# Broadcasting a softmax maximum: a transfer to all partitions and a ScalarE copy to PSUM instead of a VectorE shuffle

## The chip, the cores and the metric

The kernel runs on one core of one Trainium2 chip, all of it in 32-bit floats. The metric is the device time of one execution in microseconds (us). A core has several engines that work beside each other, each on its own list of instructions in a fixed order: TensorE (PE; its weight loads are shown apart as PEld) for matmuls and transposes, VectorE (DVE), ScalarE (ACT) and GpSimd (POOL) for elementwise work, and SyncE (SP), which here issues the transfers (DMAs). An engine waits where the next instruction in its list needs something that another engine or a transfer has not finished. SBUF is the memory with 128 partitions that all of them read and write. PSUM is the smaller memory into which TensorE writes; VectorE and ScalarE read and write it too.

## What is computed

The reference is a network of two layers over 16 batches of 64 latent vectors of 128 numbers. Each layer adds three things to the latents `x`:

```python
x = x + L0_xattn(ctx_1024, layernorm(x), ...)   # cross-attention: 16 heads of 64, 1601 context rows a batch
x = x + L0_attn(layernorm(x), ...)              # a selective scan over the 64 latents, state 16
x = x + L0_ffn(layernorm(x), ...)               # small attention over heads, then 8 experts, 2 taken, and a shared one
x = x + L1_xattn(ctx_1024, layernorm(x), mask, ...)   # the same attention with a mask over the context
x = x + L1_attn(layernorm(x), ...)              # convolution and a scan with a state of 64
x = x + L1_ffn(layernorm(x), ...)               # a gated feed-forward with both operands rounded to 4-bit blocks
```

The cross-attention, where most of the time goes, is

```python
q  = ln_latents @ Wq
kv = concat([ln_context, ln_latents]) @ Wkv     # 1601 + 64 keys
w  = softmax(q k^T * scale (+ mask))            # per head, over 1665 keys
x += (w @ v) @ Wo
```

A softmax over 1665 keys needs, for each query, the largest score before the exponentials are taken: `exp(s - max)`.

## The kernel before

**Groups and steps.** The projections of keys and values are folded into the queries and the output, so that the keys are the normalised context itself. The attention is cut into 64 groups, one for each layer, batch and half of the heads; a group has 8 heads of 64 queries, that is 512 columns (`NQ`). The 1600 first context rows and the 64 latents make 13 key tiles (`NT`) of up to 128 rows; context row 1601 is handled apart. A step is one key tile of one group, and the steps of all groups follow each other without a break: 64 x 13 of them, about 29.8 us for the 13 of one group.

In each step `scores` issues one matmul of 128 keys by 512 queries into one of three PSUM buffers `s` (L726). VectorE folds it into a running maximum `R` (128x512) with L734 (masked, layer 1) or L736 (layer 0). ScalarE copies it to an SBUF buffer `st` (L739 or L741). These buffers hold two tiles each, and there are 13 pairs of them (`PAIRS`). The exponentials come later, once the group's maximum is known: `weigh` subtracts the maximum `mb` from one pair on VectorE (L834) and takes the exponential on ScalarE (L835). `LAG` = 23 steps after a score step, `average` multiplies its weights with the values (`av`, L847, 128 queries by 129 columns, the last column being the sum of the weights). The second pair of query blocks runs one step after the first.

**From `R` to `mb`.** `R` holds, for each of 128 rows of a key tile, the maximum per query; what is left is the maximum over the 128 partitions, the same number wanted on every partition. The tuple `plan` says at which step after a group's last score (its offset) each part of that is issued:

- offset 0, `partial`: VectorE reduces `R` with a transpose in blocks of 32 into 128x16 (`part`). A second instruction (L772) joins it with the score of the apart row (`sx`) into `four`, four copies side by side, 128x64.
- offset 2, `joint`: TensorE transposes `four`, VectorE reduces it to `top`, 64x32: the 512 maxima, four times.
- offset 3, `handed`: two transfers on SyncE, `top` into every 32nd partition of `R`, and a quarter of `top` into DRAM (`mdram`).
- offset 5, `everywhere`: VectorE's stream_shuffle (L793) spreads partition 0 of each 32 over its block, from `R` into PSUM (`mb`).
- offset 7, `own_max`: a transfer reads `mdram` back as one number for each query on the partition of that query, `m4`.
- offset 11, `apart_weight`: VectorE takes `df` = score of the apart row minus `m4` (L807), ScalarE its exponential `ee`.
- offset 12, `apart_part`: GpSimd multiplies the apart row's values (`xeb`) by `ee` into `aq`, to which `gather` later adds the averages.

`weigh` begins at offset `WAIT` = 6 and takes one of the seven pairs every second step. The scores of the apart row are made for two batches at a time by `apart_scores`: VectorE copies them to `se`, adds the mask in layer 1, and spreads them into the four-fold `sx` (L477). The last group of all has another path (`maximum`, `spread_max`), and ends in `finish`.

**The other work.** It is cut into generators that hand back control after a few instructions, by `yield` with a number (a cost, charged against a budget per step) or with `HOP1`, `HOP`, `HOP3`, `HOP5` (wait 1, 2, 3 or 5 steps). A list `prep` holds what must be ready at a step: folding of weights (`fold_qk`, `fold_vo`), normalised latents, queries, and `context`, which loads and normalises a batch's context. `context` also makes its transposed form in layer 0: ScalarE writes a scaled copy into a staging tile `kts` (one buffer), and a transfer takes it to DRAM (`xhT`). `blocks` stages a group's transposed result in another tile of the same size, `tq`. A list `between` holds the scan and feed-forward of each layer (`scan0`, `moe`, then `scan1`, `ffn`), run one at a time; the first may begin `LAG` + 11 steps after the score steps that it depends on began. `scan1` and `ffn` of layer 1 run over chunks of 128 latents (two batches): chunks 0-1, 2-3, 4-5, 6 and 7. In `scan1`, for each of the chunks, four products of `bT` and `cT` go to PSUM (`gr`, L1405), from which VectorE makes `gm` (L1408).

**What sets the order.** `scores` records its own instructions on each engine (`place`). Work issued under `behind()` is ordered after the newest of these on its engine, or the one before it. A scheduler then settles the final order on each engine from the dependences, these additional ones, and its own model; every engine executes that order as it stands. SyncE issues all transfers in its order, and a transfer whose data is not ready holds those behind it. After the last group, `upto_sums` takes what is first in `between` (the last chunk but one) to the sum at the end of its `ffn`; `finish` closes the last group; and the remaining generators run alternately (`tails`). The last chunk's attention output is summed at L930, its scan's projection at L1051, its feed-forward at L1560. `fill` adds matmuls without use to keep TensorE busy there.

## Time and profile before

| what | us |
|---|---|
| median of three runs | 1907.09 |
| the three runs | 1906.38, 1907.09, 1911.22 |
| the profiled execution's own time | 1906.72 |
| its span on the engines | 1905.0 |
| TensorE (PE) busy | 1856.2 (97%) |
| VectorE (DVE) busy | 1654.1 (87%) |
| ScalarE (ACT) busy | 1325.3 (70%) |
| GpSimd (POOL) busy | 582.0 (31%) |
| granted TensorE clock, mean | 0.997 |
| bytes by DMA | 145.16 MB |

The profile is one execution, recorded by the hardware. The span runs from the first to the last instruction, and the execution's own time has 1.7 us around it. "Busy" is the sum of the time in which an engine executes; weight loads overlap matmuls. In lines on single instructions, L736 is a line of the kernel's code, the names are output and inputs, "128x512 f32" is partitions by elements. In square brackets or after `<-` stands how long the engine was idle just before, and which engine's instruction ended that wait. The granted clock says at which share of its full speed TensorE was allowed to run. The page's costliest groups are these (busy time and mean ns of one, then idle time before, and what ended it):

```profile
L847 PE MATMUL av<-kv,st 128*128 128x129 f32 x6656 | 886.4, 276 | 4.0 <-DVE aq L853 1.9
L726 PE MATMUL s<-qT,kvT 128*128 128x512 f32 x1664 | 863.0, 601 | 19.9 <-ACT st L741 9.6
L835 ACT ACTIVATE st<-st 128x1024 f32<-128x1024 f32 (+1 forms) x448 | 444.3, 995 | 123.8 <-DVE st L834 120.9
L834 DVE TENSOR_TENSOR st<-st,mb 128x1024 f32<-128x1024 f32 (+1 forms) x448 | 503.5, 1130 | 1.8 <-PE mb L821 1.1
L739 ACT ACTIVATE st<-s,mcol 128x512 f32<-128x512 f32 x416 | 283.0, 683 | 229.6 <-DVE R L734 213.6
L741 ACT COPY st<-s 128x512 f32<-128x512 f32 x416 | 238.9, 580 | 93.2 <-DVE R L736 87.7
```

The two attention matmuls take 1749 of TensorE's 1856 us. VectorE's subtraction of `mb` (L834) is its largest item with 503.5 us.

### The profile page before, as it was taken

Reading aid. Unit: us, or ns where it says so; the run is one execution under the profiler, and the core shown is the slowest. Engines: PE = TensorE matmul, PEld = TensorE weight load, DVE = VectorE, ACT = ScalarE, POOL = GpSimd, SP = SyncE. Lnnn points to the kernel's source line nnn. Section 1 sums busy time; section 2 is a strip of 40 time slices with the busy share of each in tenths; the row PEclk is TensorE's granted clock in tenths of the full one; section 3 lists DMA queues with packets and bytes.
Section 4 is the critical chain, followed back from the end, with each engine's and each line's share of the span. In section 5 each row is a group of like instructions: output and inputs, shape, how many; then the busy total and the mean of one; then the engine's idle time right before and its main releaser. Section 6 shows DMA issues by size and latency. Waiting matters only on the chain.

```text
span 1905.0 us, 32600 instructions
## 1 busy us (share of the span) xinstructions
PE 1856.2 (97%) x11494; PEld 1398.6 (73%) x11494; DVE 1654.1 (87%) x3124; ACT 1325.3 (70%) x2575; POOL 582.0 (31%) x657
## 2 busy tenths in 40 slices
PE   9999999999999999999998999999999999999997
PEld 5677777677777767777676777767777777787786
DVE  6998787998888998986999988999888987988974
ACT  5789888897878888765665756767655665665651
POOL 5222223653214553221453311455210222202110
PEclk9999999999999999999999999999999999999999
DMA  6132333442235442242433322333332132212100
GB/s 195 43 82 72 78 78 98 109 94 68 57 96 115 98 90 70 77 131 64 94 89 73 78 61 52 102 86 71 78 81 64 34 77 54 55 41 61 39 18 23
DMA packets 395886, 145.16 MB, mean 76 GB/s; under 512 B 251455, under 2 KB 386379, under 8 KB 395723
## 3 DMA queue, kind: packets, MB, share of 16 engines
q1 hardware_dynamic: 395178, 142.82, 31.4%
q8 instruction: 91, 1.49, 0.3%
q14 instruction: 73, 0.59, 0.1%
q10 hardware_dynamic: 544, 0.26, 0.0%
HBM read 97.66 MB, written 43.79 MB: 74 GB/s over the span
## 4 chain that ended last, share of the span: by engine, by line
PE 56%; DVE 9%; issue 4%; DMA 3%; ACT 1%; POOL 1%; SPq 0%; DVEq 0%; POOLq 0%; ACTq 0%
PE av L847 22%; PE s L726 21%; DVE R L734 2%; PE o L926 2%; DVE st L834 2%; PE q L518 2%; DVE h L1027 1%; PE gu L1175 1%; PE me L1160 1%; PE gu L1174 1%; DVE R L736 1%; DMA kv<-xh 1%; PE sb L1361 1%; DMA xhT<-kts 1%; DMA bb<-bcd 1%
## 5 line engine op out<-in xcount | busy, mean ns | idle before, releaser
L847 PEld LDWEIGHTS av<-kv,st 128*128 128x128 f32 x6656 | 870.3, 192 | 364.5 <-issue 343.8
L847 PE MATMUL av<-kv,st 128*128 128x129 f32 x6656 | 886.4, 276 | 4.0 <-DVE aq L853 1.9
L726 PE MATMUL s<-qT,kvT 128*128 128x512 f32 x1664 | 863.0, 601 | 19.9 <-ACT st L741 9.6
L835 ACT ACTIVATE st<-st 128x1024 f32<-128x1024 f32 (+1 forms) x448 | 444.3, 995 | 123.8 <-DVE st L834 120.9
L834 DVE TENSOR_TENSOR st<-st,mb 128x1024 f32<-128x1024 f32 (+1 forms) x448 | 503.5, 1130 | 1.8 <-PE mb L821 1.1
L739 ACT ACTIVATE st<-s,mcol 128x512 f32<-128x512 f32 x416 | 283.0, 683 | 229.6 <-DVE R L734 213.6
L741 ACT COPY st<-s 128x512 f32<-128x512 f32 x416 | 238.9, 580 | 93.2 <-DVE R L736 87.7
L734 DVE SCALAR_TENSOR_TENSOR R<-s,mcol,R 128x512 f32<-128x512 f32 x352 | 260.6, 740 | 46.4 <-PE s L726 45.3
L736 DVE TENSOR_TENSOR R<-s,R 128x512 f32<-128x512 f32 x352 | 239.8, 681 | 64.7 <-PE s L726 63.0
L726 PEld LDWEIGHTS s<-qT,kvT 128*128 128x128 f32 x1664 | 254.4, 191 | 41.5 <-ACT st L741 18.3
L644 POOL TENSOR_TENSOR kv<-kv,vec 128x384 f32<-128x384 f32 (+1 forms) x128 | 133.5, 1059 | 200.6 <-PE kt L705 85.1
L892 POOL TENSOR_TENSOR aq<-aq,rd 128x512 f32<-128x512 f32 x63 | 71.7, 1138 | 191.0 <-DVE rd L891 122.5
L1033 POOL TENSOR_TENSOR sc_y<-sc_y,h 128x512 f32<-128x512 f32 x60 | 79.4, 1323 | 127.5 <-DVE h L1032 110.5
L1016 POOL TENSOR_TENSOR db<-sc_u,bb 128x512 f32<-128x512 f32 x64 | 83.5, 1307 | 80.9 <-DVE h L1027 74.1
L1027 DVE TENSOR_TENSOR_SCAN h<-da,db 128x512 f32<-128x512 f32 x64 | 91.8, 1434 | 2.3 <-POOL db L1016 2.3
L695 ACT ACTIVATE kv<-kv,coff,crstd 128x128 f32<-128x128 f32 x182 | 78.7, 492 | 1.5 <-POOL coff L692 1.3
L815 POOL TENSOR_TENSOR aq<-xeb,ee 128x516 f32<-128x516 f32 x63 | 66.8, 1060 | 32.9 <-ACT ee L808 32.8
L686 ACT ACTIVATE scr<-kv,cmean 128x128 f32<-128x128 f32 x182 | 72.6, 399 | 3.9 <-DVE cmean L682 2.1
L641 POOL MEMSET kv<- 128x13 f32 x30 | 3.7, 125 | 218.9 <-PE av L847 218.1
L518 PE MATMUL q<-xnT,wqk 128*128 128x128 f32 x512 | 67.9, 276 | 1.0 <-ACT qT L527 0.7
L518 PEld LDWEIGHTS q<-xnT,wqk 128*128 128x128 f32 x512 | 62.6, 192 | 3.8 <-issue 1.4
L139 POOL TENSOR_TENSOR crstd<-cvar,neghalf 128x13 f32<-128x13 f32 x14 | 34.2, 2440 | 101.3 <-DVE cvar L690 101.1
(433 smaller groups left out, 1877.5 us busy)
## 6 DMA issues: line engine op xcount, KB each, us to landing
bb<-bcd SPq DMA_DIRECT2D x64, 256.0 KB
aTd<-tq SPq DMA_DIRECT2D x248, 64.0 KB
aT<-aTd SPq DMA_DIRECT2D x62, 256.0 KB
xh<-kv SPq DMA_DIRECT2D x16, 832.0 KB
kv<-xh SPq DMA_DIRECT2D x16, 832.0 KB
kvT<-xhT SPq DMA_DIRECT2D x16, 800.0 KB
kv<-in_ctx_dram SPq DMA_DIRECT2D x15, 768.0 KB
xhT<-kts SPq DMA_DIRECT2D x45, 256.0 KB
```

Source lines behind the costliest of these rows:

```text
L518: nc.tensor.matmul(t[:, k * P:(k + 1) * P], self.wqk[:, g * 4 + k, :], xnT, start=True, stop=True)
L644: nc.gpsimd.tensor_tensor(kv[:, lo:hi, :D], kv[:, lo:hi, :D], self.row(self.vec[:, w1, :], [P, hi - lo, D]), ALU.mult)
L726: mm = nc.tensor.matmul(s, self.kv_of[lay, b][1][:, i * P:(i + 1) * P], q, start=True, stop=True)
L734: mx = nc.vector.scalar_tensor_tensor(R, s, mc, last, ALU.add, ALU.max)
L736: mx = nc.vector.tensor_tensor(R, s, last, ALU.max)
L739: ev = nc.scalar.activation(st, s, AF.Identity, bias=mc)
L741: ev = nc.scalar.copy(st, s)
L834: nc.vector.tensor_tensor(st, st, self.row(mb, [P, n, NQ]), ALU.subtract)
L835: nc.scalar.activation(st, st, AF.Exp)
L847: nc.tensor.matmul(grp["av", j][:, k, :], st, self.kv_of[lay, b][0][:, i, :], start=(i == 0 and k == 0), stop=(i == NT - 1 and k == 1))
L1016: nc.gpsimd.tensor_tensor(db, u, self.row(bb[:, 0], both), ALU.mult)
L1027: nc.vector.tensor_tensor_scan(flat(h), flat(da), flat(db), 0.0, ALU.mult, ALU.add)
```

## The change

- `four` becomes `joined`, 128x16 instead of 128x64, and `top` has 16 rows instead of 64 (two buffers).
- `handed` moves from offset 3 to 2 and only writes `top` to `mdram`. The transfer into `R` is gone, and `R` has one buffer instead of two.
- `everywhere` moves from offset 5 to 2. It is now a transfer that reads the 512 numbers of `mdram` into all 128 partitions of a new SBUF tile `wide` (256 KB, one buffer).
- a new part, `settle`, at offset 6: ScalarE copies `wide` to the PSUM tile `mb`. The stream_shuffle is gone.
- `own_max` moves from offset 7 to 4. `df` becomes a part of its own, `apart_below`, at offset 9 and on GpSimd; `apart_weight` at 11 is only the exponential.
- `sx`, and in layer 1 the mask's addition to `se`, move from VectorE to GpSimd.
- `weigh` begins one step later (`WAIT` 7), `average` too (`LAG` 24), and with `LAG` the start of the work in `between`.
- `fold_vo`'s sum over the heads (L366) is made in four pieces, one step apart.
- `kts` and `tq` share one tag with two buffers.
- `scan1` hands back for two more steps (`HOP`) after the `gr` products of each chunk, except in the last scan.

```diff
--- before.py
+++ after.py
@@ -52,8 +52,8 @@
 NEG = -1.0e30
 NT = G + 1
 NQ = 512
-LAG = 23
-WAIT = 6
+LAG = 24
+WAIT = 7
 PAIRS = 13
 BLK = 32
 LOWEST = -3.0e38
@@ -363,7 +363,9 @@
         raw = lambda name: self.at.tile([P, D], F32, tag="raw", name=f"{name}{lay}", bufs=3)
         ws, b = raw("ws"), raw("b1r")
         nc.gpsimd.tensor_copy(b, self.vcol[:, b1:b1 + 1].to_broadcast([P, D]))
-        nc.vector.tensor_reduce(ws, self.wvo.rearrange("p h d -> p d h"), AX.X, ALU.add)
+        for lo in range(0, D, 32):
+            nc.vector.tensor_reduce(ws[:, lo:lo + 32], self.wvo[:, :, lo:lo + 32].rearrange("p h d -> p d h"), AX.X, ALU.add)
+            yield HOP1
         yield HOP
         t = self.tp(f"cb{lay}")
         nc.tensor.matmul(t[:, :D], b, ws, start=True, stop=True)
@@ -471,10 +473,10 @@
             for i in range(2):
                 nc.vector.tensor_copy(se[i * L:(i + 1) * L, :], mine[:, i])
             if lay:
-                nc.vector.tensor_scalar(se, se, self.mex[:, 2 * c + j:2 * c + j + 1], None, ALU.add)
+                nc.gpsimd.tensor_scalar(se, se, self.mex[:, 2 * c + j:2 * c + j + 1], None, ALU.add)
             sx = self.sm([P, H // 2, 4], "sx")
             shape = [P, H // 2, 4]
-            nc.vector.tensor_tensor(sx, self.bc(se, shape), self.row(self.own, shape), ALU.add)
+            nc.gpsimd.tensor_tensor(sx, self.bc(se, shape), self.row(self.own, shape), ALU.add)
             self.se_of[lay, 2 * c + j] = se, sx
         yield 0.6
@@ -703,7 +705,7 @@
                 t = self.tp(f"kt{b}_{g}")
                 for k in range(4 * g, min(4 * g + 4, n)):
                     nc.tensor.transpose(t[:, (k - 4 * g) * P:(k - 4 * g + 1) * P], kv[:, k, :D], self.ident)
-                raw = self.at.tile([P, 512], F32, tag="kts", name=f"kts{b}_{g}", bufs=1)
+                raw = self.at.tile([P, 512], F32, tag="kts", name=f"kts{b}_{g}", bufs=2)
                 for to, by in ((kvT[:, g * 512:g * 512 + w], w1), (raw[:, :w], YG1)):
                     nc.scalar.activation(to, t[:, :w], AF.Copy, scale=self.vcol[:, by:by + 1])
                 nc.sync.dma_start(out=self.xhT[b][:, g * 512:g * 512 + w], in_=raw[:, :w])
@@ -716,7 +718,7 @@
         lay, b, half = grp["key"]
         if i == 0:
             grp["st"] = []
-            grp["R"] = self.at.tile([P, NQ], F32, tag="R", name=f"R{g}", bufs=2)
+            grp["R"] = self.at.tile([P, NQ], F32, tag="R", name=f"R{g}", bufs=1)
         if i % 2 == 0:
             n = min(2, NT - i)
             grp["st"].append(self.at.tile([P, n, NQ], F32, tag=f"st{n}", name=f"st{g}_{i // 2}", bufs=PAIRS if n == 2 else 2))
@@ -767,30 +769,34 @@
         lay, b, half = grp["key"]
         sx = self.se_of[lay, b][1][:, half * 4:half * 4 + 4, :].rearrange("p k f -> p (k f)")
         t = grp["turn"] = self.tp(f"tm{g}")
-        part, four = t[:, P:P + 16], self.sm([P, 4, 16], "four", bufs=2)
+        part, joined = t[:, P:P + 16], self.sm([P, 16], "joined")
         nc.vector.tensor_reduce(part, grp["R"].rearrange("p (c j) -> p c j", j=BLK), AX.X, ALU.max, apply_transpose=True)
-        nc.vector.tensor_tensor(four, self.row(part, [P, 4, 16]), self.row(sx, [P, 4, 16]), ALU.max)
-        grp["four"] = four.rearrange("p r c -> p (r c)")
+        nc.vector.tensor_tensor(joined, part, sx, ALU.max)
+        grp["joined"] = joined
     def joint(self, g):
         nc, grp = self.nc, self.groups[g]
         t = grp.pop("turn")
-        nc.tensor.transpose(t[:64, :P], grp["four"], self.ident)
-        top = grp["top"] = self.sm([64, BLK], "top")
-        nc.vector.tensor_reduce(top, t[:64, :P].rearrange("c (a j) -> c j a", j=BLK), AX.X, ALU.max)
+        nc.tensor.transpose(t[:16, :P], grp["joined"], self.ident)
+        top = grp["top"] = self.sm([16, BLK], "top", bufs=2)
+        nc.vector.tensor_reduce(top, t[:16, :P].rearrange("c (a j) -> c j a", j=BLK), AX.X, ALU.max)
     def handed(self, g):
-        nc, grp = self.nc, self.groups[g]
-        nc.sync.dma_start(out=grp["R"][0:P:BLK, :], in_=grp["top"])
-        nc.sync.dma_start(out=self.mdram[g], in_=grp["top"][:16])
+        grp = self.groups[g]
+        self.nc.sync.dma_start(out=self.mdram[g], in_=grp["top"])
     def everywhere(self, g):
+
+        wide = self.groups[g]["wide"] = self.at.tile([P, NQ], F32, tag="wide", name=f"wide{g}", bufs=1)
+        self.nc.sync.dma_start(out=wide, in_=self.mdram[g].rearrange("c j -> (c j)").partition_broadcast(P))
+
+    def settle(self, g):
         grp = self.groups[g]
         grp["mb"] = self.tp(f"mb{g}")
-        self.nc.vector.stream_shuffle(grp["mb"], grp["R"], [0] * BLK)
+        self.nc.scalar.copy(grp["mb"], grp.pop("wide"))
     def own_max(self, g):
@@ -799,14 +805,18 @@
         with nc.allow_non_contiguous_dma(reason="one number for each query"):
             nc.sync.dma_start(out=m4, in_=self.mdram[g].rearrange("(k f) j -> (f j) k", k=4))
+    def apart_below(self, g):
+
+        grp = self.groups[g]
+        lay, b, half = grp["key"]
+        df = grp["df"] = self.sm([P, 4], "df")
+        self.nc.gpsimd.tensor_tensor(df, self.se_of[lay, b][0][:, half * 4:half * 4 + 4], grp["m4"], ALU.subtract)
+
     def apart_weight(self, g):
-        nc, grp = self.nc, self.groups[g]
-        lay, b, half = grp["key"]
-        df, ee = self.sm([P, 4], "df"), self.sm([P, 4], "ee")
-        nc.vector.tensor_tensor(df, self.se_of[lay, b][0][:, half * 4:half * 4 + 4], grp["m4"], ALU.subtract)
-        nc.scalar.activation(ee, df, AF.Exp)
-        grp["ee"] = ee
+        grp = self.groups[g]
+        ee = grp["ee"] = self.sm([P, 4], "ee")
+        self.nc.scalar.activation(ee, grp.pop("df"), AF.Exp)
     def apart_part(self, g):
@@ -894,7 +904,7 @@
     def blocks(self, g):
         nc, aq = self.nc, self.groups[g]["aq"]
-        t = self.at.tile([P, NQ], F32, tag="tq", name=f"tq{g}", bufs=1)
+        t = self.at.tile([P, NQ], F32, tag="kts", name=f"tq{g}", bufs=2)
         nc.vector.transpose(t.rearrange("p (k d) -> p k d", k=4), aq[:, :, :D])
         for i in range(P // BLK):
             to = self.aTd[g].rearrange("(j r) (k i c) -> i r k j c", r=BLK, i=P // BLK, c=BLK)[i]
@@ -1407,6 +1417,8 @@
                     gi = gm[c].rearrange("p (k i) t -> p i k t", i=2)[:, i]
                     nc.vector.tensor_tensor(gi, gs[i][:, :2 * L].rearrange("p (k t) -> p k t", k=2), self.row(self.upto, [P, 2, L]), ALU.mult)
                 yield 0.6
+                if not last:
+                    yield HOP
             for c in range(CG):
                 sg = self.tp(f"seg{c}")
                 for h in range(NH):
@@ -1570,7 +1582,7 @@
         self.groups = [{"key": (lay, b, half)} for lay in range(2) for b in range(NB) for half in range(2)]
         ng = len(self.groups)
         self.plan = (
-            ((0, self.partial), (2, self.joint), (3, self.handed), (5, self.everywhere), (7, self.own_max), (11, self.apart_weight), (12, self.apart_part)),
+            ((0, self.partial), (2, self.joint), (2, self.handed), (2, self.everywhere), (4, self.own_max), (6, self.settle), (9, self.apart_below), (11, self.apart_weight), (12, self.apart_part)),
             ((1, self.maximum), (3, self.spread_max)),
         )
         per_layer = NB * 2 * NT
```

## The prediction

> **What bounds the kernel now.** I read the page's busy times first, then stretches of the span, then the waits, then the two ends of the chain of waits.
>
> ```profile
> PE 1856.2 (97%) x11494; PEld 1398.6 (73%) x11494; DVE 1654.1 (87%) x3124; ACT 1325.3 (70%) x2575; POOL 582.0 (31%) x657
> ```
>
> TensorE is the bound almost throughout: 1856.2 of 1905.0 us. A change that leaves the matmuls alone (this one does: 5996 issued before and after) can win only from the other 49 us and from matmuls run slowly. Where is that time? The next fence is the table of stretches (us; then busy us of PE, its weight load, DVE, ACT, POOL; granted clock; DMA).
>
> ```profile
> 340.00:450.00 110.00, 106.14 (x630) 78.97 (x628) 107.25 (x170) 95.88 (x223) 61.60 (x55) 1.00 0.42 92
> 600.00:720.00 120.00, 113.41 (x666) 83.89 (x665) 114.01 (x173) 103.21 (x232) 64.36 (x59) 1.00 0.46 104
> 910.00:1050.00 140.00, 128.98 (x731) 92.30 (x730) 131.17 (x189) 86.55 (x142) 63.55 (x56) 0.99 0.35 77
> 1250.00:1320.00 70.00, 65.85 (x369) 46.88 (x368) 69.91 (x109) 48.22 (x77) 43.80 (x38) 1.00 0.44 93
> 1830.00:1905.00 75.00, 64.43 (x499) 55.48 (x498) 42.56 (x122) 19.97 (x42) 8.07 (x14) 1.00 0.09 22
> 1604.20:1607.60 3.40, 3.40 (x16) 1.86 (x14) 2.03 (x4) 2.23 (x4) 0.00 (x0) 0.50 0.27 43
> ```
>
> The first four are the stretches with `scan0` beside the attention: VectorE is 94 to 100% busy and TensorE idles 3.9+6.6+11.0+4.1 = 25.6 us. The fifth is the end, 10.6 us idle. The sixth is a stretch at half clock; the waits before it, and the waits that tie TensorE to VectorE:
>
> ```profile
> ACT st L739 <- DVE R L734: 213.6, 203, 3.5
> ACT st L741 <- DVE R L736: 87.7, 98, 3.2
> PE s L726 <- ACT st L741: 9.6, 17, 1.1
> 1602.76 0.31 PEld L1405 LDWEIGHTS gr<-sd_cT,sd_bT 64*64 64x64 f32 x8 [2.04 <-DVE gm L1408]
> 1721.90 0.51 PEld L1405 LDWEIGHTS gr<-sd_cT,sd_bT 64*64 64x64 f32 x16 [2.86 <-DVE gm L1408]
> ```
>
> A score matmul needs one of three PSUM buffers; ScalarE's eviction frees it and waits for VectorE's running maximum. So VectorE's backlog reaches TensorE through ScalarE. The two `gr` lines are `scan1`, second pair of batches, waiting for VectorE's `gm`.
>
> **The change part by part.** The profiled execution took 1906.7 us (span 1905.0), 0.4 below the median of 1907.1; the sum is made against 1906.7.
>
> **VectorE relief.** These rows are every execution of a line (min/median/max ns).
>
> ```profile
> L793 DVE STREAM_SHUFFLE mb<-R x63: 677/690/692, 46.0 to 1816.9; 128x512 f32<-128x512 f32 x63
> L807 DVE TENSOR_TENSOR df<-se,m x63: 125/156/1016, 54.5 to 1831.4; 128x4 f32<-128x4 f32 x63
> L772 DVE TENSOR_TENSOR four<-tm,sx x63: 152/204/225, 40.2 to 1806.7; 128x64 f32<-128x64 f32 x63
> L477 DVE TENSOR_TENSOR sx<-se,own x32: 177/193/1168, 38.2 to 1720.0; 128x32 f32<-128x32 f32 x32
> ```
>
> Per group VectorE loses 0.69 (shuffle) + 0.16 (`df`) + 0.05 (`joined` on 16 columns instead of 64) = 0.9 us, and per batch one `sx` (0.19) and in layer 1 one `se` add (0.22): about 1.05 us a group, 67 us in all. Only where VectorE is the limit does that move the end. The four stretches hold 440/29.8 = 14.8 groups, so 15.5 us of VectorE. I take two thirds, 10 us, since some of the 25.6 idle us there has other causes. Ends: -4 (one quarter) and -16 (all of it).
>
> **Steps in `scan1`.** Two extra steps after each half's `gr` put the second half's `gr` four to five score steps after the first's, in the first two scans (order of the changed kernel); in the third both stay in one step. The gaps cost TensorE about 2 us each (the weight loads waited 2.04 and 2.86, partly behind running matmuls), and 3 us later follow 3.4 us at half clock (0.50 above), 1.7 us each: 7.5 us. I take -7, ends 0 and -7.5. "TensorE: Matmul & The Clock Gate" of the Trainium skill, section "Why this matters for your kernels", asks for no idle gaps over about 3 us. By it, 2-us gaps are safe and this part would be worth only 4; the half-clock rows decide against it here.
>
> **Shared staging and the split sum.** One `kts` buffer made ScalarE wait for the transfer out of it: two pieces of the chain, 3.4 and 7.1 us, cost TensorE three gaps of about 0.9. With two buffers: -2 (ends 0, -2.7). The 3.66 us sum over `wvo` (L366) becomes four of about 0.92 with evictions' maxima between; TensorE waited 0.85 us for it at 1015.9 and paid some more for the backlog: -2 (ends 0, -3.7).
>
> **GpSimd.** It takes `df`, `sx` and `se`. In every group the GpSimd instruction that will precede `df` ended, in this trace, at least 3.2 us before the exponential `ee` that waits for `df`; the number it needs landed 3.8 us or more ahead. Cost 0; if that cover went, ScalarE would stand still at `ee`, with evictions behind it. `sx` took 1.09 and 1.17 us on VectorE beside GpSimd's `kv` products at 1719.96 and 1023.11, against 0.18 alone, so leaving VectorE also removes such waits (inside the relief above). "SBUF — State Buffer", section "SBUF: two separate sides", says GpSimd and VectorE share a port pair that the first comer holds; that speaks against the move. Read so, 111 new GpSimd instructions could block VectorE instead, some 5 us in the four stretches (an estimate at 0.2 us each). By the rule the sum would be 1905; I leave it out.
>
> **Transfer and copy.** The 8 KB into `R` goes, a 256 KB broadcast comes: one DMA each, so SyncE issues as many. The broadcast waits on SyncE for `mdram`'s write, median 1.5 us; queued behind it are `own_max`, `aT`, `bb` and `xeb`, all with steps to spare. No row shows the broadcast; nearest is `bb` (256 KB to all partitions), by its landings 4.4 to 8.2 us, median 5.1 (the other end: 2.1 for `kts` out). `top` to `wide` is then 1.5+5.1+0.6 = 7.2 us, 12 when an `xh` of 832 KB (4.8 us) goes in between. In the changed order ScalarE's copy comes after eviction 6 to 9; in this trace's times 8.2 to 18.3 us after `top`, median 11.8. It is hidden mostly. The copy itself is 0.59 us (an eviction of that size), 37 us in all, on the path only where ScalarE is: 15 contexts, up to 9 us. I take +2 (ends 0, +9).
>
> **Weighing later.** The subtractions stand on VectorE after the running maximum of step 8.6 on average (6.0 before); TensorE needs the first pair at step 12 (11 before). From step 9 that leaves three steps, 6.6 us, for lag 1.6 + subtraction 1.13 + exponential 1.0: hidden. In eight groups they stand after step 10, and in the first after 11: up to 1.5 us each. Up to five subtractions (5.7 us) now follow each other; the three PSUM buffers cover that. +3 (ends 0, +12). A shorter life of the 13 buffer pairs by one step still leaves two.
>
> **The end.** LAG+1 and the extra steps leave `scan1` of the seventh chunk a dozen steps behind at the last score. The changed order puts its projection after the last average and all of that chunk's `ffn` between the last group's third and fourth transpose. Before, most of it ran beside the averages:
>
> ```profile
> 1861.44 0.15 DVE L867 TENSOR_TENSOR den<-av,ee 128x2 f32<-128x2 f32 x1
> 1869.03 0.29 DVE L1560 TENSOR_TENSOR X<-X,fo 128x128 f32<-128x128 f32 x1 [2.56 <-PE fo L1555]
> 1870.21 0.29 DVE L930 TENSOR_TENSOR X<-X,o 128x128 f32<-128x128 f32 x1 [0.89 <-PE o L926]
> 1887.90 0.29 DVE L1051 TENSOR_TENSOR X<-X,po 128x128 f32<-128x128 f32 x1 [0.82 <-PE po L1047]
> 1902.17 0.29 DVE L1560 TENSOR_TENSOR X<-X,fo 128x128 f32<-128x128 f32 x1 [1.88 <-PE fo L1555]
> ```
>
> From `den` to the last attention sum (L930) it is 8.8 us. It becomes 1.3 to the projection's sum, 14.3 for the chunk's `ffn` (the last chunk's, L1051 to L1560), 1.2 to L930: 16.8. Of the 8.0 more, 1.9 return because projection, `fg` and `fu` no longer stand before `den`. Added: about 1.5 of half clock in a stretch without fills and 1.5 of TensorE waiting for `scan1` among the averages. +9 (ends +5, +14).
>
> Sum: -10 -7 -2 -2 +2 +3 +9 = -7: 1900 us.
>
> **The rivals.** *The relief buys nothing* (no faster): TensorE's gaps stay because ScalarE is the limit (103 of 120 us busy in the second stretch) and now has the copy too. For it: ScalarE waits little there at 694 to 714 us. Against: 301 us of its waiting for VectorE. Without 7 of the 10: 1907. *The transfer comes late* (slower): broadcasts queue behind `xh` and `bb`, ScalarE stands at the copy, evictions back up. It decides from (7+5.7)/63 = 0.2 us of TensorE lost per group; with 0.27 a group it gives 1900+17 = 1917. For it: transfers under load took up to 8.2 us. Against: the copy's median turn of 11.8. *The end stays covered or the relief counts in full* (faster): +5 and -15 for those two terms and the others as summed, 1890.7. For it: VectorE at 94 to 100% in the four stretches. Against: ScalarE at 86% in the second.
>
> **How the numbers follow.** About 0.3% (5.7 us) is what a measurement can tell from no change: 1901.4 to 1912.8 is the same. My sum has 0.45 and straddles the lower bound: 0.32 faster, 0.13 same. No relief 0.22 (0.03, 0.14, 0.05). Late transfer 0.17, all slower. Better end 0.16, all faster. Faster 0.51, same 0.27, slower 0.22. The sum's own range, each term half-way to its ends and added as independent (root of the sum of squares), is 1896 to 1908; the 8-in-10 range takes in the rivals: 1888 to 1916.
>
> **What would show it.** Right: VectorE busy near 1587 us, ScalarE near 1362; TensorE's idle in the four stretches down by some 10; no `gr` wait of 2 us; `den` to L930's counterpart near 17 us. Wrong: waits of ScalarE's `mb` copy on `wide`; more TensorE wait on evictions than before; half-clock stretches in new places; an end as short as before.

## The result, and the profile after

The changed kernel takes 1928.9 us, the median of six runs (1924.7 to 1932.5). The kernel before took 1908.5 beside them (1905.0 to 1912.3). The ratio is 1.0113, with a 95% interval of 1.0094 to 1.0132: slower by 1.1%, where 1900 was forecast and 1916 was the upper end of the range.

The profiled execution took 1931.6 us, its span is 1929.9. First the page of the changed kernel: busy time, and two rows of the DMA issues (KB each, median us from issue to landing).

```profile
PE 1860.7 (96%) x11494; PEld 1396.9 (72%) x11494; DVE 1594.6 (83%) x2893; ACT 1349.6 (70%) x2638; POOL 612.7 (32%) x768
...
bb<-bcd SPq DMA_DIRECT2D x64, 256.0 KB, 5.0
wide<-md SPq DMA_DIRECT2D x63, 256.0 KB, 4.2
```

VectorE's busy time fell by 59.5 us and ScalarE's rose by 24.3. The 63 new copies on ScalarE take 37.2 us; busy time counts instructions that overlap only once. TensorE's busy time grew by 4.5 us with the same 11494 instructions: its mean granted clock is 0.994, where it was 0.997, so more of its work ran at a lower clock. The whole span grew by 24.9.

Next the stretches (us; then busy us of PE, its weight load, DVE, ACT, POOL; granted clock; DMA): the four that were shown of before, then the time from the last score's eviction to the end, and 18 us within that.

```profile
340.00:450.00 110.00, 103.54 (x610) 76.31 (x609) 101.20 (x149) 93.98 (x213) 63.62 (x61) 1.00 0.45 105
600.00:720.00 120.00, 112.58 (x657) 83.66 (x656) 104.10 (x153) 103.60 (x231) 64.87 (x60) 0.97 0.46 108
910.00:1050.00 140.00, 129.69 (x754) 93.65 (x753) 127.11 (x182) 91.85 (x150) 65.61 (x68) 1.00 0.40 98
1250.00:1320.00 70.00, 65.89 (x366) 46.23 (x366) 67.14 (x98) 48.41 (x79) 39.72 (x42) 1.00 0.48 112
1844.30:1930.00 85.70, 68.68 (x518) 58.87 (x516) 48.03 (x137) 23.65 (x52) 7.97 (x15) 0.91 0.08 19
1877.00:1895.00 18.00, 8.92 (x38) 6.34 (x38) 8.79 (x26) 2.24 (x7) 0.84 (x3) 0.67 0.03 10
```

In the four stretches VectorE's busy time fell from 422.3 to 399.6 us, by 22.8. TensorE's idle time in them did not fall: 25.6 us before, 6.5 + 7.4 + 10.3 + 4.1 = 28.3 now. But the changed kernel falls behind, so the same stretch of time holds other work. To compare the same work I bounded the four stretches by the same score evictions in both traces. Here are the sums over the four, first of the kernel before, then of the changed one:

```profile
sum 443.10, PE 417.46 PEld 305.46 DVE 425.77 ACT 336.89 POOL 235.44; mean PE 104.37 PEld 76.37 DVE 106.44 ACT 84.22 POOL 58.86
sum 447.30, PE 418.12 PEld 303.21 DVE 410.23 ACT 343.20 POOL 246.27; mean PE 104.53 PEld 75.80 DVE 102.56 ACT 85.80 POOL 61.57
```

For the same work VectorE is busy 15.5 us less, and TensorE's idle time rises from 25.6 to 29.2 us. In the last row of the table TensorE is busy half the time, at two thirds of its clock.

To see where time goes I set the two traces side by side by progress: the start of ScalarE's eviction of the last score of each group. The last of all is at 1833.9 us before and at 1844.3 after (+10.4); from there to the end of the span it is 71.1 before and 85.6 after (+14.5). These two numbers, "last eviction" and "end", stand in the table of runs below. They are read from one execution each, and the executions of one kernel differ by some us. The waits of the changed kernel (us in total, times, longest):

```profile
ACT st L741 <- DVE R L736: 206.6, 217, 3.8
ACT st L743 <- DVE R L738: 110.0, 108, 3.9
...
ACT mb L799 <- DMA wide<-md: 20.4, 13, 3.1
...
DVE st L844 <- ACT mb L799: 17.9, 20, 3.0
```

ScalarE's wait for VectorE's running maximum, 301.3 us before (213.6 + 87.7), is 316.6 now, with less VectorE work. Two waits are new: ScalarE's copy waits 13 times for the broadcast, and 20 times the first subtraction waits for the copy.

### The profile page after: what moved, and what is told of

It reads as the page before. It is cut to its first block, busy times and chain, and to the rows that moved or that the text cites. A ratio compares the mean times of both kernels' runs of the same rounds, so it can differ in the third digit from the quotient of the medians.

```text
span 1929.9 us, 32696 instructions
## 1 busy us (share of the span) xinstructions
PE 1860.7 (96%) x11494; PEld 1396.9 (72%) x11494; DVE 1594.6 (83%) x2893; ACT 1349.6 (70%) x2638; POOL 612.7 (32%) x768
## 2 busy tenths in 40 slices
DMA packets 400675, 161.17 MB, mean 84 GB/s; under 512 B 248179, under 2 KB 383103, under 8 KB 400511
## 4 chain that ended last, share of the span: by engine, by line
PE 41%; DVE 9%; issue 4%; DMA 2%; ACT 1%; POOL 1%; SPq 0%; DVEq 0%; POOLq 0%; ACTq 0%
PE av L857 16%; PE s L728 15%; DVE R L736 3%; DVE st L844 2%; PE o L936 1%; PE q L520 1%; DMA wide<-md 1%; PE gu L1184 1%; PE me L1170 1%; PE gu L1185 1%; PE sb L1371 1%; DVE h L1037 0%; PE fo L1567 0%; DVE tm L773 0%; ACT st L845 0%
## 5 line engine op out<-in xcount | busy, mean ns | idle before, releaser
L813 POOL TENSOR_TENSOR df<-se,m 128x4 f32<-128x4 f32 x63 | 15.0, 238 | 268.7 <-DMA m<-md 265.7
L936 PEld LDWEIGHTS o<-wvo,aT 128*128 128x128 f32 x512 | 59.9, 193 | 6.7 <-issue 3.3
```

## The experiments

Every row is one kernel, compared with the kernel before on the same chip. "Last eviction" and "end" are us of the profiled execution against the 1833.9 and 71.1 of the kernel before.

| kernel | median us | ratio to before (95%) | last eviction | end |
|---|---|---|---|---|
| changed | 1928.9 | 1.0113 (1.0094 to 1.0132) | +10.4 | +14.5 |
| before_wide: before + broadcast and copy | 1927.2 | 1.0102 (1.0087 to 1.0117) | +16.9 | +4.0 |
| after_shuffle: changed, shuffle back | 1917.6 | 1.0055 (1.0038 to 1.0072) | -5.6 | +16.2 |
| after_early: changed, broadcast made early, with another group's maxima | 1914.0 | 1.0028 (1.0015 to 1.0041) | -8.5 | +15.6 |
| after_sp: changed, broadcast first on the queue | 1939.9 | 1.0161 (1.0137 to 1.0184) | +17.5 | +15.0 |
| before_hop: before + steps in scan1 | 1911.0 | 1.0020 (1.0010 to 1.0030) | -5.1 | +13.7 |
| after_nohop: changed without them | 1921.0 | 1.0070 (1.0051 to 1.0088) | +14.3 | +3.5 |
| before_lag: before + LAG 24, WAIT 7 | 1923.6 | 1.0068 (1.0049 to 1.0086) | +15.6 | +1.6 |
| before_wait7: before + WAIT 7 | 1910.4 | 1.0007 (0.9992 to 1.0022) | +5.8 | +3.6 |
| before_lag24: before + LAG 24 | 1920.8 | 1.0068 (1.0049 to 1.0088) | +10.9 | +3.0 |
| before_lag_phase: before_lag, other work not later | 1916.7 | 1.0040 (1.0029 to 1.0051) | +8.3 | +1.1 |
| after_lag: changed with LAG 23, WAIT 6 | 1918.0 | 1.0045 (1.0029 to 1.0062) | -2.8 | +13.8 |
| gp_lag22: before_gp with LAG 22 | 1901.4 | 0.9966 (0.9954 to 0.9977) | -2.8 | -2.5 |
| before_small: before + split sum, staging, sx and se on GpSimd | 1896.2 | 0.9929 (0.9905 to 0.9954) | -10.4 | +1.3 |
| before_gp: before + sx and se on GpSimd | 1894.7 | 0.9919 (0.9903 to 0.9936) | -14.1 | 0.0 |
| after_dve: changed, sx, se and df on VectorE | 1933.8 | 1.0131 (1.0110 to 1.0151) | +12.4 | +14.6 |
| best2a: before_small + steps after the first gr only | 1893.8 | 0.9921 (0.9902 to 0.9940) | -17.6 | +4.1 |
| gp_hop: the same without split sum and staging | 1896.4 | 0.9935 (0.9920 to 0.9950) | -15.0 | +4.1 |
| best_df: best2a + df on GpSimd | 1896.1 | 0.9941 (0.9924 to 0.9958) | -14.7 | +3.1 |

An edit does more than its own lines say: the scheduler settles the order on each engine anew. With the moved instructions left aside, at least 3% of VectorE's instructions stand elsewhere in its order in before_gp than in the kernel before, 13% in after_early than in the changed kernel, and 26% in before_lag24 than in the kernel before. So a row is the price of an edit together with the order that came of it.

### The broadcast and the copy

Two runs: the transfer and copy alone in the kernel before, and the shuffle put back into the changed one.

```diff
 before_wide (on the kernel before; partial, joint, handed, everywhere and settle as in the change)
-(0, self.partial), (2, self.joint), (3, self.handed), (5, self.everywhere), (7, self.own_max), (11, self.apart_weight)
+(0, self.partial), (2, self.joint), (2, self.handed), (2, self.everywhere), (4, self.own_max), (6, self.settle), (11, self.apart_weight)
-        grp["R"] = ..., bufs=2)
+        grp["R"] = ..., bufs=1)
 after_shuffle (on the changed kernel; partial, joint, handed and everywhere as before, R with two buffers)
-(2, self.handed), (2, self.everywhere), (4, self.own_max), (6, self.settle), (9, self.apart_below)
+(3, self.handed), (5, self.everywhere), (7, self.own_max), (9, self.apart_below)
```

> The kernel before with only the broadcast and ScalarE's copy in the place of the shuffle (offsets of the changed kernel for joint to settle, df still on VectorE, LAG 23 and WAIT 6). Theory (late broadcast): ScalarE waits 20 us or more for it, since weighing begins one step earlier than in the changed kernel, and the kernel takes 1915 to 1925 with the end at 71 us. Rival (VectorE's relief of 0.7 us a group counts and the broadcast is hidden): 1897 to 1905.

> The changed kernel with the shuffle on VectorE and its two transfers back in the place of the broadcast and ScalarE's copy (R with two buffers again, offsets 3, 5 and 7 as before); everything else as changed. Theory (the broadcast lands late and ScalarE stands at the copy with evictions behind it): ScalarE's 20 us of waiting for the broadcast go, the 3.5 us gap of TensorE near 690 us and the half clock after it go, and the last score comes 8 to 14 us earlier: 1915 to 1921. Rival (the later LAG and the shifted order of the other work cost it, the broadcast is hidden): 1929, or up to 10 more since VectorE gets its 42 us back.

The broadcast costs 20 us alone (1.0102) and 11 in the changed kernel (1.0055 against 1.0113). Both went the way of the theory of a late broadcast, before_wide 2 us beyond its range. In before_wide, the waits of ScalarE and VectorE:

```profile
ACT mb L797 <- DMA wide<-md: 30.1, 16, 3.6
...
DVE st L838 <- ACT mb L797: 30.2, 22, 3.7
```

How a late landing reaches TensorE is seen at one place of the changed kernel, in the timeline (start us, us, engine, instruction, in brackets the idle time before and what ended it):

```profile
683.21 0.42 SPq L793 DMA_DIRECT2D wide<-md  x1
...
688.61 0.59 ACT L799 COPY mb<-wide 128x512 f32<-128x512 f32 x1 [1.85 <-DMA wide<-md]
...
689.24 2.35 DVE L844 TENSOR_TENSOR st<-st,mb 128x1024 f32<-128x1024 f32 x2 [1.09 <-ACT mb L799]
...
692.43 1.04 ACT L743 COPY st<-s 128x512 f32<-128x512 f32 x2
...
693.05 3.78 PE L728 MATMUL s<-qT,kvT 128*128 128x512 f32 x4 [3.30 <-ACT st L743]
```

The broadcast lands 5.4 us after its issue. ScalarE stands for 1.85 us with other work (the context's `scr`, `da`) and two evictions behind the copy, and catches up at 692.43. TensorE's next score, which needs an evicted buffer, comes 3.30 us late, and TensorE ran at half clock from 691.9 to 698.7 us.

Where is the lateness from? By the landing events of this trace the broadcast lands a median of 8.8 us after `top`, 16.7 at most: the write of `mdram` is issued 1.1 us after `top` (behind the four `aTd` transfers on SyncE's queue) and the broadcast 4.2 us after `top`. In between the queue waits for `mdram`'s write to land and in 41 of the 63 groups also holds `aT`, which waits for `aTd`. Two more runs took these causes apart.

```diff
 after_early (on the changed kernel)
-  (2, everywhere): wide <- mdram[g]
+  (8, everywhere_next): wide of group g + 1 <- mdram[g]
 after_sp (on the changed kernel)
   dma = nc.sync.dma_start(out=wide, in_=mdram[g] to all partitions)
+  self.place["SP"].append(dma.ins)
```

> The changed kernel with the broadcast made eight steps after the end of the group before, and from that group's maxima: as many transfers of the same size and as many copies, but nothing to wait for. (The numbers subtracted are then those of another group, so this leaves the computation of the right maximum out of the broadcast; nothing else is left out.) Theory (waiting for the landing is the price): ScalarE's 20 us of waits for the broadcast go, the last score comes 8 to 16 us earlier, with the end unchanged at 85 to 87 us: 1913 to 1921. Rival (the 63 copies on ScalarE, the traffic and the later weighing are the price): 1925 to 1931.

> The changed kernel with one ordering added on SyncE's queue: whatever is issued later than the broadcast under behind() stays behind it, so that the read of aTd (aT) and the 832 KB xh no longer stand between the write of mdram and the broadcast. Theory (the broadcast is late because it queues behind aT, which waits for aTd): its issue comes from a median of 3.9 us after top to about 2.9, its landing from 8.5 to about 7, ScalarE's waiting for it from 20 us to under 8, and the kernel from 1929 to 1918 to 1924. Rival (the transfers' own times are what is late, not the queue): ScalarE still waits 15 us or more and the time stays at 1926 to 1931.

With the same 63 transfers and copies but nothing to wait for, the kernel takes 15 us less than the changed one (1.0028 against 1.0113), and ScalarE's wait for the broadcast is 1.2 us in total. (The numbers that it subtracts are another group's, so it leaves out the right maximum.) So the price is the waiting, as far as another order does not share in it; neither the traffic nor ScalarE's 37 us of copies is. The sum over the four stretches, bounded by the same evictions, shows what VectorE's relief is worth once nothing waits for the broadcast:

```profile
sum 435.40, PE 416.36 PEld 306.47 DVE 409.96 ACT 345.75 POOL 245.97; mean PE 104.09 PEld 76.62 DVE 102.49 ACT 86.44 POOL 61.49
```

TensorE is idle 19.0 us, 6.6 less than in the kernel before and 10.1 less than in the changed one.

The second run refuted my remedy. The broadcast was issued a median of 3.1 us after `top` and landed at 6.6, and ScalarE's wait for it fell from 20.4 to 7.0 us; yet the kernel got 11 us slower. Its timeline at 936 to 952 us shows what stood on the queue instead:

```profile
936.25 0.56 SPq L788 DMA_DIRECT2D md<-top  x1
...
937.98 0.33 SPq L793 DMA_DIRECT2D wide<-md  x1
...
938.36 1.46 SPq L1016 DMA_DIRECT2D bb<-bcd  x3
...
944.46 2.49 POOL L1027 TENSOR_TENSOR db<-sc_u,bb 128x512 f32<-128x512 f32 x2 [11.55 <-DMA bb<-bcd]
...
945.75 3.38 DVE L1038 TENSOR_TENSOR_SCAN h<-da,db 128x512 f32<-128x512 f32 x2 [2.41 <-POOL db L1027]
...
950.66 0.74 DVE L736 SCALAR_TENSOR_TENSOR R<-s,mcol,R 128x512 f32<-128x512 f32 x1
...
951.44 0.69 ACT L741 ACTIVATE st<-s,mcol 128x512 f32<-128x512 f32 x1 [2.41 <-DVE R L736]
...
952.18 2.08 PE L728 MATMUL s<-qT,kvT 128*128 128x512 f32 x2 [6.72 <-ACT st L741]
```

`bb`, which `scan0` needs, is issued after `mdram`'s write and the broadcast. GpSimd waits for it, VectorE's scan waits for GpSimd, the next running maximum stands behind the scan, then the eviction, then TensorE: 6.7 us. Over that whole kernel GpSimd waited 29.3 us (7 times) for `bb` at this line, against 1.1 (twice) in the changed kernel. Making one transfer earlier on an ordered queue made another one late.

### The extra steps in scan1, and the end

```diff
 before_hop (on the kernel before); after_nohop (on the changed kernel) takes the two lines out
                 yield 0.6
+                if not last:
+                    yield HOP
             for c in range(CG):
```

> The kernel before with only the two extra steps in scan1. Theory (the steps remove the gr waits and lengthen the end): the two gr waits of 2 us and the half clock after them go, the last score's eviction comes some 7 us earlier, and the end grows from 71 to about 85 us: about 1914. Rival (the steps alone don't delay the last scans enough): the end stays at 71 us and the kernel gains the 7 us: 1900.

> The changed kernel without the two extra steps in scan1; all else as changed. Theory (the extra steps push the last scans into the end): in the order written for TensorE, ffn of the last chunk but one stands beside the last group's averages again, so the time from the last score's eviction to the end goes from 85.6 us back to about 71, and the kernel from 1929 to about 1918 (14.5 less, 4 back for the two gr waits that return). Rival (LAG one step later is what lengthens the end): the end stays at 84 to 86 us and the kernel at 1929 or above.

The steps do both things. Alone they bring the last eviction 5.1 us earlier, and between 1560 and 1760 us no wait of `gr` is left. They also lengthen the end by 13.7 us; taking them out of the changed kernel shortens it from 85.6 to 74.6. (The profiled executions of before_hop and after_nohop took 4.2 and 3.5 us more than their medians, so these columns are that much too high in sum: by the medians the steps cost the kernel before about 4 us, not 8.6.) In the changed kernel the end looks like this: the same four sums that were shown of before, in the order that they have now (`den`, then the projection and the `ffn` of the seventh chunk, then the last attention sum), with two matmuls between.

```profile
1875.52 0.16 DVE L877 TENSOR_TENSOR den<-av,ee 128x2 f32<-128x2 f32 x1 [0.22 <-PE av L857]
...
1875.96 0.29 DVE L1061 TENSOR_TENSOR X<-X,po 128x128 f32<-128x128 f32 x1
...
1882.17 0.86 PE L1543 MATMUL fg<-wgT,ff_xT 128*128 128x352 f32 x2 [0.48 <-ACT ff_xT L184]
...
1889.03 1.08 PE L1560 MATMUL ft<-ident,hb 128*88 128x128 f32 x4 [5.07 <-DVE hb L1499]
...
1892.89 0.29 DVE L1572 TENSOR_TENSOR X<-X,fo 128x128 f32<-128x128 f32 x1 [3.92 <-PE fo L1567]
...
1894.68 0.29 DVE L940 TENSOR_TENSOR X<-X,o 128x128 f32<-128x128 f32 x1 [1.50 <-PE o L936]
```

`den` to the last attention sum is 19.2 us, where it was 8.8. TensorE stands 5.07 us in one piece, and the clock is halved for 13.6 us from about 1883.

### Averaging later

```diff
 before_lag (on the kernel before)          before_wait7: WAIT alone; before_lag24: LAG alone
-LAG, WAIT = 23, 6
+LAG, WAIT = 24, 7
 before_lag_phase (on before_lag)
-done = lambda lay, b: start(lay, b) + LAG + 11
+done = lambda lay, b: start(lay, b) + LAG + 10
 after_lag (on the changed kernel): LAG 23, WAIT 6
 gp_lag22 (on before_gp): LAG 22, WAIT 6
```

> The changed kernel with LAG 23 and WAIT 6 as before; all else as changed. Theory (late broadcast): with weighing one step earlier there is less room, ScalarE and VectorE wait 30 us or more for the broadcast's copy and TensorE more for the averages: 1930 to 1938, with the end at 84 us or more. Rival (the later LAG shifts the other work against the context's and makes the collisions near 782 and 813 us): these two gaps go, and the kernel takes 1918 to 1924.

I had put after_lag in to confirm the late broadcast, and it went the other way: with less room, and 25.3 us of ScalarE waiting for the broadcast, the kernel was 11 us faster than the changed one. So the shift by one step costs by itself.

> The kernel before with only LAG 24 and WAIT 7, the shuffle kept. Theory (weighing and averaging one step later crowd VectorE's subtractions together and shift the scans and feed-forwards, which cost the changed kernel 10 us by the run without it): the last score comes some 10 us later, the end stays at 71 to 74 us: 1914 to 1920. Rival (the later LAG only hurts together with the late broadcast): 1905 to 1909.

> The kernel before with LAG 24 and WAIT 7, but the work in between started LAG + 10 steps after its scores instead of LAG + 11, so at the same steps as in the kernel before. If the start of the scans and feed-forwards one step later is what costs: back to 1905 to 1909. If the later weighing and averaging themselves cost (five subtractions in a row, averages that come due beside other work): it stays with the run that has LAG 24 and WAIT 7 alone, 1914 to 1920.

> The kernel before with only WAIT 7 (weighing one step later), LAG 23. Theory (the later subtractions fall in a row among the running maxima, and evictions wait for those): most of the 15 us that WAIT 7 and LAG 24 cost together stays: 1915 to 1922, the end at 71 us. Rival (the later averages and their beat against the other work cost): 1905 to 1911.

> The kernel before with only LAG 24 (averages, and the start of the scans and feed-forwards, one step later), WAIT 6. If weighing later is the price: 1907 to 1912, of which 2 in the end. If the averages' beat and the shifted start are: 1914 to 1922.

LAG and WAIT together cost the kernel before 0.68%, about 13 us. WAIT alone can't be told from nothing (1.0007, interval 0.9992 to 1.0022), so subtractions in a row are not the reason that I took them for. (Its profiled execution took 1916.1, 5.7 above its median; its last two columns in the table are high for that.) LAG alone costs as much as both (1.0068). About 0.3% of it seems to come from the scans and feed-forwards that start a step later: with their start put back it is 1.0040, though the two intervals just overlap. In before_lag these waits grew (before: 87.7, 3.3 and 2.1 us):

```profile
ACT st L741 <- DVE R L736: 119.5, 122, 3.7
...
ACT kts L708 <- DMA xhT<-kts: 9.8, 9, 2.9
...
PEld tm L779 <- DVE four L772: 8.0, 9, 1.4
```

They are spread over many places, and which of them carries the rest of the loss I have not settled.

> The kernel before with se and sx on GpSimd and LAG 22 (WAIT 6). Later averages cost 13 us; if that is because averages in the later position meet other work more, an earlier position may meet less: 1885 to 1893, below the 1894.7 of the same kernel with LAG 23, the end about 2 us shorter. If 23 is the position in which the pieces happen to fit and any shift costs: 1900 to 1910.

One step earlier costs too: 0.9966 against the 0.9919 of the same kernel with LAG 23. So of the three values tried 23 is the best, as if the rest of the order were fitted to it; that it is so fitted is not shown.

### The small parts

```diff
 before_gp (on the kernel before); before_small also has the sum in four pieces and kts, tq in two buffers
-nc.vector.tensor_scalar(se, se, mex...)        nc.vector.tensor_tensor(sx, se, own)
+nc.gpsimd.tensor_scalar(se, se, mex...)        nc.gpsimd.tensor_tensor(sx, se, own)
 after_dve (on the changed kernel): these two and df back on nc.vector
```

> The kernel before with the sum of fold_vo in four pieces, kts and tq in one tag of two buffers, and se and sx on GpSimd; no other part of the change. By the prediction's terms: 2 for the staging, 2 for the sum, 1 to 3 for 0.2 to 0.4 us less of VectorE a batch: 1900 to 1904, with the end at 71 us. Rival (none of these waits was on a path, GpSimd's instructions cost what they save): 1906 to 1909.

> The kernel before with only se's addition and sx on GpSimd. Of the 11 us that this, the shared staging and the sum in four pieces gave together, the prediction's terms put 4 on the staging and the sum: if the rest is VectorE's relief and the sx that waited beside GpSimd, 1899 to 1902; if GpSimd's part buys nothing and the staging and the sum were undervalued, 1905 to 1908.

> The changed kernel with sx, se's addition and df back on VectorE; all else as changed. If GpSimd's part is worth its 14 us in the changed kernel as in the one before: 1938 to 1945, with sx taking up to 1 us on VectorE beside GpSimd. If it is worth that only where a stretch at half clock hung on it (the gr products, which the extra steps take care of here): 1928 to 1934.

All the gain of before_small is in `se` and `sx` (0.9919 alone, 0.9929 with the others), and it is the largest gain of the whole change. VectorE does 13.9 us less by it (1654.1 to 1640.2), and the kernel takes 14 to 15 us less. Why so much for 48 small instructions? A part of it shows in the kernel before at its first `gr` wait:

```profile
1596.65 4.34 POOL L644 TENSOR_TENSOR kv<-kv,vec 128x512 f32<-128x512 f32 x4 [1.04 <-DVE sx L477]
...
1598.32 0.94 DVE L477 TENSOR_TENSOR sx<-se,own 128x32 f32<-128x32 f32 x1
...
1599.30 0.75 DVE L734 SCALAR_TENSOR_TENSOR R<-s,mcol,R 128x512 f32<-128x512 f32 x1
...
1602.43 0.27 DVE L1408 TENSOR_TENSOR gm<-gr,upto 128x128 f32<-128x128 f32 x1
```

`sx` takes 0.94 us on VectorE while GpSimd runs its `kv` products; its median is 0.19. Behind it stand the running maximum, four more instructions and then `gm`, for which TensorE waits. All eight of the 32 `sx` that took 0.65 us or more ran beside a GpSimd product. Over the kernel, the 32 `sx` take 12.3 us on VectorE and 8.1 on GpSimd, where the longest takes 0.51. In the kernel before three stretches of 3.4 us at half clock begin at 993, 1604 and 1724 us; in before_gp none is left before the last few us, which is worth 5.1 us (half of each). Of the 14 us, 3.0 arise between 1022 and 1036 us of the old trace, where a `se` and two `sx` took 0.80, 1.17 and 0.90, and 5.0 between 1566 and 1750 us, where two `sx` took 0.94 and 1.09 and the last two stretches lie.

Not all of the gain comes from these waits. Another 3.4 us arise between 986 and 1005 us, with the first stretch at half clock, and there is no `se` or `sx` in the old trace from 908 to 1022 us. What differs there is VectorE's order: a subtraction that stood behind the scan in the kernel before stands ahead of it in before_gp. TensorE's wait for it, before and in before_gp:

```profile
992.35 0.71 PE L345 MATMUL WvT<-rawWo,rawWvT 64*128 64x128 f32 x4 [1.63 <-DVE st L834]
...
989.57 0.79 PE L345 MATMUL WvT<-rawWo,rawWvT 64*128 64x128 f32 x8 [0.69 <-DVE st L834]
```

So the 14 us are the price of the move and of the order that the scheduler then chose; how they divide over the whole kernel is open.

"SBUF — State Buffer" of the Trainium skill, section "SBUF: two separate sides", says that a VectorE instruction with two inputs in SBUF and a GpSimd instruction that reads SBUF exclude each other for the whole instruction; a `sx` of 0.94 us beside a `kv` product agrees with that. I had read the rule as speaking against the move. The small instruction on VectorE was the one that waited.

In the changed kernel the part is worth 5 us (1.0131 without it, 1.0113 with it, intervals that overlap). There the extra steps already take care of the `gr` waits, and in after_dve the 32 `sx` on VectorE take only 6.3 us, the longest 0.51: in that order they meet few of GpSimd's products.

> The kernel before with the three small parts (sum in four pieces, shared staging, se and sx on GpSimd) and with two extra steps in scan1 only after the first of a pair's two gr products, none in the scans of one chunk. Theory (parts add up, the end depends on how many steps scan1 is delayed): the small parts give 11 as alone, the gr waits go (5 us by the last score), and the last chunk but one is half as late, its ffn's first two products before the last group's second transpose: an end of 72 to 78 us, 1890 to 1896. Rival (any delay of the scans costs the whole 14 us at the end): 1900 to 1905.

> The kernel before with only se and sx on GpSimd and two extra steps in scan1 after the first of a pair's two gr products. Staging and sum as before. Theory (the staging and the sum in four pieces bring nothing beside GpSimd's part, which gave 14 alone): 1889 to 1895. Rival (they bring their 2 each): 1896 to 1899, above the 1893.8 of the run that has them too.

> The kernel before with the three small parts and two extra steps after the first of a pair's gr products (1893.8 so far), and with df on GpSimd at offset 9 as in the changed kernel. By the prediction's step (GpSimd's instruction ahead of df ends at least 3.2 us before ee, cost 0; 0.16 us of VectorE less a group): 1888 to 1894. Rival (df waits on GpSimd for the transfer of m with the scan's and the context's products behind it): 1897 to 1904.

```diff
 best2a (on before_small); gp_hop has it on before_gp
                 yield 0.6
+                if CG > 1 and not c:
+                    yield HOP
 best_df (on best2a): df on GpSimd at offset 9, its exponential at 11
```

With the steps only between the two `gr` products of a pair, added to before_small, the last eviction comes 17.6 us earlier (10.4 without them) and the end grows by 4.1 instead of 13.7. Added to before_gp they bring 0.9 us there and cost 4.1 at the end (0.9935 against 0.9919, intervals that overlap). best2a and before_gp are the two best kernels, 0.9921 and 0.9919: 0.8% faster than the kernel before, 1.9% faster than the changed one, and not to be told apart from each other. Neither the split sum with the shared staging nor `df` on GpSimd shows a gain or a loss that these runs can resolve.

### What the parts add up to

By the ratios alone, the parts put into the kernel before are: broadcast and copy +1.02%, LAG and WAIT +0.68%, steps in scan1 +0.20%, `sx` and `se` on GpSimd -0.81%. The sum is +1.09%; the change measures +1.13%. Undone one at a time in the changed kernel the sizes differ (0.58% for the broadcast, 0.68% for LAG and WAIT, 0.43% for the steps), and these, less 0.18% for `sx`, `se` and `df`, come to 1.51%. So the agreement is in part luck.

## Why the prediction was wrong, step by step

- **VectorE relief, -10.** VectorE's busy time fell as forecast (1594.6 against "near 1587"), and for the same work in the four stretches by the 15.5 us worked out. But TensorE's idle there rose by 3.5 us instead of falling by 10. With the broadcast made early it fell by 6.6, two thirds of what I took: the relief is there, the waiting for the broadcast took it back and more. Both runs with the broadcast undone or made early show a last eviction 16 to 19 us earlier than the changed kernel's. One piece was badly under-sized: moving `sx` and `se`, 0.3 us a batch in my sum, is worth 14 us alone, in part because of where they stood and in part by the order that came of it. How the 14 divide is open. I had noted their 1.09 and 1.17 us beside GpSimd's products and left them "inside the relief".
- **Steps in scan1, -7.** Right in mechanism and nearly in size: -5.1 by the last eviction, and the two `gr` waits gone. The half clock at 993 us hung on another gap.
- **Staging and split sum, -4.** No gain shown: before_small is not faster than before_gp.
- **Transfer and copy, +2 (ends 0, +9).** This is the first step that failed, with +17 by the last eviction and +20 in all in the kernel before, and +16 and +11 in the changed one. The working said: 7.2 us from `top` to landing, the copy's turn at 11.8, "hidden mostly". The landing came at 8.8 and up to 16.7. The wait of the write behind `aTd` (1.1 us) was left out, and `aT` was listed behind the broadcast when it mostly stood ahead of it. And a median turn covers only a median landing: 13 late ones of 63 carried the loss. The rival "the transfer comes late" had the right mechanism and named its price, 0.27 us of TensorE a group: 16.9 us over 63 groups is 0.27. That it meets this number is luck, since by the medians it is 0.32 in the kernel before and 0.18 in the changed one. It was given 0.17.
- **Weighing later, +3.** What I priced, the later subtractions, is within the measurement (1.0007). What I didn't price in the body is LAG: averages, their sums and transposes, and all scans and feed-forwards one step later: +13 us. That is the second failed step, an edit of one digit taken for its slack alone. About 0.3% of the time may be due to the later start of scans and feed-forwards; the cause of the rest stays open.
- **The end, +9 (ends +5, +14).** Right in mechanism, under-sized: +14.5, of which before_hop gives 13.7, so it is the extra steps and hardly LAG. Up to `den` it is 3.7 us longer, from `den` to the last attention sum 10.4 (8.0, and 1.5 for half clock, forecast): the `ffn` of the seventh chunk took 16.9 us between its sums instead of 14.3, with the clock halved for 13.6 us.
- **GpSimd, 0.** Right for `df`: GpSimd stands 265.7 us before it (41 times) waiting for `m`, and best_df shows no cost beyond the interval. The rule that I set against the move pointed to a part of the gain, as told above.
- **The range.** The terms' upper ends, added up, reach 1937.7, and the result lies inside. I narrowed them as if independent and gave the one rival with the right mechanism 0.17.

## What to carry to other kernels

A broadcast by DMA that replaces an on-chip shuffle has to be judged by its late landings, on the queue that it shares: what stands ahead of it there, and what it makes stand behind. A tiny instruction on a busy engine is not priced by its median but by what it waits for and by who stands behind it; of 32 with a median of 0.19 us, eight took 0.65 to 1.17 here. And where an order is fitted by hand, shifting one constant by a step, or moving a few small instructions, changes the order of much else, so it needs a run of its own before other parts are built on it.

## What the runs showed of the hardware that I had not expected

In these traces the length of a gap of TensorE alone does not say whether half clock follows. In all 20 profiles, leaving out the first 50 us and the end, I took the gaps between the starts of two successive matmuls beyond what is usual for the shape. These were followed by a stretch at half clock within 3.5 us, each for 3.4 us or a multiple:

| gap, us | gaps | followed by half clock |
|---|---|---|
| 1.20 to 1.78 | 112 | 2 |
| 1.79 to 1.99 | 27 | 7 |
| 2.00 to 3.65 | 37 | 22 |
| 3.81 to 6.89 | 3 | 3 |

One of the two in the first row has another gap, of 1.89 us, right behind it, with which it shares the stretch; the other is one of 1.70 us in before_wait7. Two of the gaps in after_dve, of 1.97 and 2.30 us, share one stretch too. A gap of 3.57 us in the changed kernel at 813 us had none; one of 1.79 in the kernel before had. "TensorE: Matmul & The Clock Gate" of the Trainium skill, section "Why this matters for your kernels", asks for no gaps over about 3 us; by these runs 2 us can be enough.

The other surprise is how little the traffic mattered. The 63 broadcasts moved 16 MB more (161.17 MB against 145.16), and with them early enough (after_early) the last eviction came earlier than with the shuffle in the changed kernel (-8.5 against -5.6 us; by the ratios 1.0028 against 1.0055, intervals that just overlap).
